# A four-layer sequence of cross-attention and RWKV blocks: ten products of a constant at the start, first queries by seven block products, low-rank projections side by side on TensorE's columns

## The chip, the cores and the metric

The kernel runs on one core of one Trainium2 chip, in fp32 throughout. The metric is the device time of one execution in microseconds. The time before is the median of three runs.

## The reference

The input x has 8 sequences of 112 tokens with 512 channels (896 tokens in all); a context of 375 tokens with 512 channels belongs to each sequence. Four layers follow one another:

```python
# layer 0: one cross-attention without heads
q, k, v = x @ w_q.T, ctx @ w_k.T, ctx @ w_v.T
x = x + alpha * ((softmax(q @ k.T / sqrt(512)) @ v) @ w_o.T)

# layers 1 and 2: RWKV blocks, their states taken from ctx
xa  = LN(x);  sx = shift(xa) - xa
xx  = xa + sx * maa_x
t   = tanh(xx @ maa_w1)              # 512 -> 160, five groups of 32
m   = einsum(t by group, maa_w2)     # five times 32 -> 512
xw, xk, xv, xr, xg = xa + sx * (maa_f + m_f)       # one for each group f
w   = exp(-exp(time_decay + tanh(xw @ decay_w1) @ decay_w2))   # 512 -> 64 -> 512
r, k, v = xr @ Wr.T, xk @ Wk.T, xv @ Wv.T
g   = silu(xg @ Wg.T)
y   = scan over tokens of s = w * s + k v, read out with r     # 32 heads of 16
x   = x + (GN(y) * g) @ Wo.T
x   = x + sigmoid(xr2 @ fWr.T) * (relu(xk2 @ fWk.T)**2 @ fWv.T)

# layer 3: two cross-attentions of 16 heads of 128 channels, then an MLP of 2048
```

## The kernel before, in words

Channels lie on the partitions: x is a tile of 128 partitions by NC = 4 channel groups by N = 896 tokens. A projection is, for each half of the tokens (NH = 448 columns) and each of four output groups, four matmuls of 128x128 weights by 128x448 tokens into one PSUM bank, and an eviction by ACT or DVE. An fp32 matmul shows in the trace as two records.

**Layer 0** (`layer0`, L252) runs in an order written out by hand for PE, DVE, ACT and GpSimd; SyncE's order is chosen by the scheduler. `turned` (L314) transposes w_q and w_k on TensorE, 16 products by an identity each, four to a bank, which ACT and DVE evict in turn from two banks. `product` (L324) then multiplies the two into w_qk, scaled, so that no keys need be made: q0 = w_qk x by `project` (L167, evicted by ACT at L388), and the scores are q0 by the context itself. w_v and w_o are multiplied in the same way into w_vo. The loads go out in the order w_q, w_k, x, context, w_v, w_o. `mean_c` (128x128, all 1/512, a memset of DVE at the start) is the weight of every layer norm's mean (L188).

While that runs, `park` (L279) rearranges the contexts of two sequences into sums of blocks (copies of ACT, subtractions of GpSimd at L291) in a single buffer, tag "blocks", and SyncE puts them into DRAM. From there they are read later by a generator, `values` (L884), which makes layer 3's values: its matmuls `ps_vk` (L994, 0.86 us each, with an ACT eviction each) are work that depends on nothing in layers 1 and 2. `fill(n)` takes n steps from whichever generator is `filler` at the time, so that this work stands in the waits of those layers.

**Layers 1 and 2** (`time_mix_inputs`, L458) go through the two token halves h = 0 and 1. `mixes` makes a layer norm (part_mean and part_var by DVE, `mean_c` by PE, the square by ACT; L184 to L195), the shifted difference sx (GpSimd) and xx, four chunks by DVE at L516. Then come two sets of four matmuls (L525): w1 holds the first four groups of maa_w1 (128 output rows), w1e the fifth group of 32 four times over, filled by four DMAs, so that t1 holds it once on each quarter of the partitions. A Tanh evicts each (t4, t1). The mixing products (L534) have only 32 rows in the contraction, and four of them run beside one another on TensorE's rows; DVE evicts them (L537, L540). `projections` makes d (L552), four matmuls whose weights d1 hold the 64 columns of decay_w1 twice, td by Tanh, then in turn the gate g (L562, Silu at L570) and the decay: ps_w (L579) from td's upper and lower 64 partitions, two products beside one another, e by Exp with a bias (L583) and decay by another Exp (L584). ACT loads a table where it goes from Silu to Exp or back. The tiles e, ruk and the layer norm's part_mean and part_var share the tag "e" with two buffers. After that v, k and r are projected.

The order of this part is found by the scheduler from the program order, dependences and estimated costs. Half 0's projections are the filler of half 1's mixes:

```python
pieces = projections(0, *mixes(0, ...))
values_filler, filler = filler, pieces
following = projections(1, *mixes(1, (2, 1, 2, 1, 1, 1, 0, 0)))
```

`time_mix` is the scan: DVE multiplies and scans, GpSimd multiplies by r, and the sums over the heads' channels (L746) are matmuls with 32 output columns, four of them beside one another on TensorE's columns by `tile_position=(0, 32 * q)`. Fillers stand between them.

**Layer 3** makes its projections by `seven` (L1149): seven products of 2x2 blocks in the place of eight, from sums of blocks of the weights (`weight_sums`) and of the tokens.

Of the kernel before, what the change touches and what calls it, by code (L numbers as in the profile page):

```python
# [30 lines left out]
P = 128  # L31
# [19 lines left out]
BLOCK = 2 * CT  # L51

# [58 lines left out]
def tile_kernel(ctx: ExitStack, tc: tile.TileContext, d: dict, out: bass.AP):  # L111
# [30 lines left out]
    pick = marked.tile([P, 4, 4 * HB], F32, name="pick")  # L142
    mean_c = const.tile([P, P], F32, name="mean_c")
# [89 lines left out]
    def patterns(pool, ident):  # L233
# [10 lines left out]
        nc.vector.tensor_sub(less_mean_h, ident, mean_h)  # L244

# [4 lines left out]


    def layer0():  # L252
# [3 lines left out]
        with (  # L256
# [8 lines left out]
            ident = identity(keep, "a0")  # L265
            w_q, w_k = weight("L0_xattn_w_q"), weight("L0_xattn_w_k")
# [57 lines left out]
            def product(a, b, name, pool, tag, scale=1.0):  # L324

                y = pool.tile([P, NC, C], F32, tag=tag, name=name)
# [55 lines left out]
            with tc.manual_schedule(engines=ORDERED):  # L382
                w_qk = product(turned(w_q, "q"), turned(w_k, "k"), "w_qk", wpool, "w", 1.0 / math.sqrt(C))
                project(
                    ps,
                    w_qk,
                    lambda k, h: halves(x[:, k, :], h),
                    lambda o, h, p: nc.scalar.copy(halves(q[:, o, :], h), p),  # L388
                    "q0",
                )  # L390

                w_vo = product(turned(w_v, "v", wpool, "w"), w_o, "w_vo", last, "w_vo")
# [65 lines left out]
    def time_mix_inputs(n, pre, names, ones_t, first, k, v, r, g, decay, rows):  # L458
# [7 lines left out]
        with (  # L466
# [7 lines left out]
            w1e = one.tile([P, NC, P], F32, name=f"maa1e_{n}")  # L474
# [3 lines left out]
            for q in range(4):  # L478
                part = slice(q * DM, (q + 1) * DM)
                nc.sync.dma_start(w1e[:, :, part], d[pre + "maa_w1"][:, :, P:])  # L480
                nc.sync.dma_start(w2e[part], d[pre + "maa_w2"][P:])
# [24 lines left out]
            def mixes(h, fills):  # L506
# [15 lines left out]
                for dst, w in ((t4, w1), (t1, w1e)):  # L522
                    p = mm(ps, f"ps_t{n}_{h}_{int(dst is t1)}")[:, :NH]
                    for c in range(NC):
                        nc.tensor.matmul(p, w[:, c], xx[:, c, :], start=c == 0, stop=c == NC - 1)  # L525
                    nc.scalar.activation(dst, p, AF.Tanh)
# [21 lines left out]
            def projections(h, xw, xg):  # L548

                p = mm(ps, f"ps_d{n}_{h}")[:, :NH]  # L550
                for c in range(NC):
                    nc.tensor.matmul(p, d1[:, c, :], xw[:, c, :], start=c == 0, stop=c == NC - 1)  # L552
                td = one.tile([P, NH], F32, tag="t4", name=f"td{n}_{h}")
# [21 lines left out]
                for pair in range(2):  # L575
                    ps_w = [mm(ps, f"ps_w{n}_{h}_{o}")[:, :NH] for o in (2 * pair, 2 * pair + 1)]
                    for q in range(2):
# [537 lines left out]
    def weight_sums(pool, tag, w, u, eng=None, later=None):  # L1115
# [22 lines left out]
        for step in steps:  # L1138
            step()
# [667 lines left out]
```

## Time and profile before

| what | value |
| --- | --- |
| runs | 2889.84, 2891.95, 2893.08 us |
| median | 2891.95 us |
| profiled execution | 2892.85 us |
| its span | 2890.7 us |
| mean granted TensorE clock | 0.989 |
| busy: PE, DVE, ACT, POOL | 97%, 62%, 35%, 36% of the span |
| layer 0's first transpose, first w_qk product | 5.79 us, 13.91 us |
| q0 | 27.75 to 51.97 us |
| layer 1: variance of half 1's layer norm | 213.63 us |
| layer 2: the same | 834.28 us |

The span is the profiled execution of one core from its first to its last instruction; the profiled execution's own time holds 2.1 us more around it. Engines are PE (TensorE's matmuls), PEld (its weight loads), DVE, ACT, POOL (GpSimd) and SP (SyncE, which issues the DMAs). A group's line has the source line, the engine, the operation, out and in, the count, and behind the bar the busy time in us, the mean of one in ns, and the idle time ahead of it with what ended it. PEclk is the share of full speed that the clock gate granted to TensorE.

### The profile page before, as it was taken

The page shows a single profiled execution, that of the slowest core. Times are in us where ns is not written, and L with a number is a line of the kernel's source. Part 1 is how long each engine was busy: PE and PEld are TensorE (multiplying, and loading weights), DVE is VectorE, ACT ScalarE, POOL GpSimd, SP SyncE. Part 2 cuts the span into 40 slices and gives each one's busy share as a digit, 9 for nine tenths or more (in the row PEclk, how much of TensorE's full clock was granted, in tenths as well). Part 3 has the DMA queues.
Part 4 walks back from the last instruction along what each step waited for, and adds up shares of the span by engine and source line. Part 5 has one row for each costly group of instructions (what it writes and reads, how often), then busy time and mean ns, then how long its engine had stood idle before and what let it go on. Part 6 is the DMA issues. An engine that isn't in the chain of part 4 may idle for free.

```text
span 2890.7 us, 31049 instructions
## 1 busy us (share of the span) xinstructions
PE 2791.5 (97%) x10476; PEld 1588.2 (55%) x10476; DVE 1800.7 (62%) x2301; ACT 1012.7 (35%) x1953; POOL 1052.2 (36%) x836
## 2 busy tenths in 40 slices
PE   8989999999999999999999999999899999999999
PEld 4734443344444433347467676767476676767544
DVE  1464288856352688834457676757767676757555
ACT  2232466633243456523233232313333232313311
POOL 1432178744231487733322221313122232313030
PEclk9999999999999999999999999999999999999999
DMA  5621498944221789842435352525244352523010
GB/s 206 239 77 39 142 282 254 277 122 136 85 71 57 236 241 277 241 137 92 130 103 156 95 165 94 163 92 159 74 133 133 115 166 89 162 93 115 28 47 26
DMA packets 233310, 400.90 MB, mean 139 GB/s; under 512 B 35144, under 2 KB 170344, under 8 KB 226368
## 3 DMA queue, kind: packets, MB, share of 16 engines
q1 hardware_dynamic: 233152, 398.92, 44.1%
q8 instruction: 84, 1.38, 0.2%
q14 instruction: 74, 0.61, 0.1%
HBM read 321.06 MB, written 77.91 MB: 138 GB/s over the span
## 4 chain that ended last, share of the span: by engine, by line
PE 73%; DVE 15%; POOL 4%; ACT 4%; issue 2%; DMA 2%; SPq 0%; DVEq 0%; ACTq 0%; POOLq 0%
PE ps_vk L994 14%; PE ps_k1k L1235 8%; PE ps_k5k L1235 6%; PE av L1496 4%; PE sc L1448 4%; PE ps_o L167 3%; DVE each L1488 2%; PE ps_k1q L1162 2%; PE ps_fk L167 2%; PE ps_r L562 2%; PE ps_k L562 2%; PE ps_k5q L1162 2%; PE ps_k7q L1162 2%; PE ps_v L562 2%; PE ps_fr L167 2%
## 5 line engine op out<-in xcount | busy, mean ns | idle before, releaser
L994 PE MATMUL ps_vk<-wv,cv 128*128 128x512 f32 x1296 | 583.8, 601 | 15.4 <-ACT k L1092 9.1
L994 PEld LDWEIGHTS ps_vk<-wv,cv 128*128 128x128 f32 x1296 | 243.5, 191 | 339.8 <-issue 285.4
L1483 POOL PARTITION_ALL_REDUCE each<-tops x113 | 182.4, 1614 | 466.0 <-DVE tops L1472 464.1
L1020 POOL TENSOR_TENSOR k<-k,k 128x512 f32<-128x512 f32 (+1 forms) x153 | 197.8, 1293 | 327.0 <-ACT k L1019 276.4
L1458 POOL PARTITION_ALL_REDUCE tops<-top x128 | 139.3, 1088 | 427.5 <-DVE top L1456 417.3
L769 DVE TENSOR_TENSOR_SCAN st<-decay,kv 128x904 f32<-128x904 f32 x128 | 260.7, 2037 | 17.6 <-POOL rs L773 4.4
L773 POOL TENSOR_TENSOR rs<-st,r 128x896 f32<-128x896 f32 x128 | 247.3, 1932 | 51.6 <-DVE st L769 46.7
L1466 ACT ACTIVATE pts<-pts,rests 128x448 f32<-128x448 f32 (+1 forms) x256 | 133.2, 567 | 337.6 <-DVE pts L1464 325.9
L1496 PEld LDWEIGHTS av<-pts,v 125*128 125x128 f32 (+1 forms) x1536 | 190.9, 191 | 33.1 <-ACT pts L1466 3.9
L1448 PEld LDWEIGHTS sc<-q,k 128*128 128x128 f32 x1536 | 189.4, 192 | 33.0 <-DVE each L1488 9.4
L1448 PE MATMUL sc<-q,k 128*128 128x112 f32 x1536 | 193.0, 276 | 8.6 <-DVE each L1488 8.3
L1488 DVE RECIPROCAL each<-each 128x224 f32<-128x224 f32 x113 | 174.7, 1546 | 31.3 <-POOL each L1483 28.7
L1496 PE MATMUL av<-pts,v 125*128 125x112 f32 (+1 forms) x1536 | 190.9, 274 | 1.3 <-ACT pts L1466 1.3
L1235 PE MATMUL ps_k1k<-cs,wsk 128*128 128x375 f32 x480 | 173.6, 483 | 6.5 <-ACT u2k L1237 5.3
L765 DVE TENSOR_TENSOR kv<-vp,k 128x904 f32<-128x904 f32 x128 | 141.5, 1105 | 60.5 <-ACT vp L667 55.3
L1019 ACT COPY k<-ps_vk 128x512 f32<-128x512 f32 (+1 forms) x153 | 89.2, 583 | 179.6 <-PE ps_vk L994 176.8
L1092 ACT COPY k<-ps_vk 128x512 f32<-128x512 f32 (+1 forms) x153 | 89.1, 583 | 172.9 <-PE ps_vk L994 163.7
L1456 DVE TENSOR_REDUCE top<-sc 128x224 f32<-128x672 f32 x128 | 109.1, 852 | 28.6 <-PE sc L1448 28.6
L667 ACT COPY vp<-vj 128x896 f32<-128x896 f32 x124 | 112.8, 910 | 9.3 <-DMA vj<-rows 5.4
L1464 DVE TENSOR_TENSOR pts<-sc,tops 128x672 f32<-128x672 f32 x128 | 102.8, 803 | 17.6 <-POOL tops L1458 17.6
L1235 PEld LDWEIGHTS ps_k1k<-cs,wsk 128*128 128x128 f32 x480 | 84.0, 189 | 51.3 <-ACT u2k L1237 7.6
L1237 ACT COPY p1k<-ps_k1k 128x375 f32<-128x375 f32 x60 | 27.9, 465 | 212.1 <-PE ps_k1k L1235 212.1
(416 smaller groups left out, 4788.6 us busy)
## 6 DMA issues: line engine op xcount, KB each, us to landing
vj<-rows SPq DMA_DIRECT2D x124, 448.0 KB
cv<-blocks SPq DMA_DIRECT2D x181, 251.5 KB
cs<-blocks SPq DMA_DIRECT2D x120, 375.0 KB
wvs<-k SPq DMA_DIRECT2D x128, 256.0 KB
v<-wvs SPq DMA_DIRECT2D x128, 256.0 KB
cx<-in_ctxT SPq DMA_DIRECT2D x38, 750.0 KB
v<-wvs SPq DMA_DIRECT2D x128, 126.0 KB
wvs<-k SPq DMA_DIRECT2D x64, 224.0 KB
```

Source lines behind the costliest of these rows:

```text
L167: nc.tensor.matmul(p, w[:, k, o * P : (o + 1) * P], rhs(k, h), start=k == 0, stop=k == NC - 1)
L562: nc.tensor.matmul(y, ws[f][:, c, o * P : (o + 1) * P], x_f, start=c == 0, stop=c == NC - 1)
L769: nc.vector.tensor_tensor_scan(flat(st), flat(decay[:, c]), flat(kv), 0.0, ALU.mult, ALU.add)
L773: nc.gpsimd.tensor_mul(by_batch(rs), st[:, :, :L], by_batch(r[:, c, :]))
L994: nc.tensor.matmul(to, left, right, start=start and n == 0, stop=k == 1, skip_group_check=True)
L1020: nc.gpsimd.tensor_add(y, z, y)
L1162: nc.tensor.matmul(to, lhsT, rhs, start=start and k == 0, stop=k == 1, skip_group_check=not start)
L1235: nc.tensor.matmul(y, lhsT, rhs, start=start and k == 0, stop=k == 1, skip_group_check=True)
L1448: nc.tensor.matmul(sc[:, t, y * L : (y + 1) * L], kt[:, o, t * CT : t * CT + P], q[:, o, b * L : (b + 1) * L], start=True, stop=True,)
L1483: nc.gpsimd.partition_all_reduce(each, it[4], P, ReduceOp.add)
L1488: nc.vector.reciprocal(each, sums)
L1496: nc.tensor.matmul(av[:, y], v[:nt, t, y * HD : (y + 1) * HD], pts[:nt, t, y * L : (y + 1) * L], start=t == 0, stop=t == 2,)
```

## The change

There are six edits.

- Ten matmuls of mean_c by mean_c into a PSUM bank that nothing reads stand first on PE.
- q0 is made by `seven` in the place of `project`. The token sums lie in z (free until the attention), the weight sums in w_vo (filled only afterwards), and p1, u2, u3 in a tile `parts0` of the tag "blocks". `seven` and its helpers move up in the file; `weight_sums` takes a tile, and `tile_of` a function, for that.
- A tile `folded` holds the sum of the identity's four column quarters: 128 rows by 32 columns.
- w1e holds the fifth group once (one DMA). Each of the four channel chunks' products goes to a column tile of 32 columns of its own, and so to its own quarter of the partitions of one bank; ACT copies them, and four products with `folded` on four column tiles sum the chunks and repeat the sum on each quarter; Tanh follows. They stand ahead of t4's four matmuls and after them.
- d is made on two column tiles of 64 columns, each with one half of the 448 tokens, so that td has 224 columns with the first tokens above and the last below.
- ps_w takes four products of 224 columns in the place of two of 448 for each pair of channel groups, and each Exp at L583 becomes two of 224 columns.

```diff
+START = 10
...
+    folded = marked.tile([P, DM], F32, name="folded")
...
+        nc.vector.tensor_add(folded, ident[:, :DM], ident[:, DM : 2 * DM])
+        for q in range(2, 4):
+            nc.vector.tensor_add(folded, folded, ident[:, q * DM : (q + 1) * DM])
...
             ident = identity(keep, "a0")
+            start = mm(ps, "ps_start")
+            for _ in range(START):
+                nc.tensor.matmul(start[:, :P], mean_c, mean_c, start=True, stop=True)
...
                 w_qk = product(turned(w_q, "q"), turned(w_k, "k"), "w_qk", wpool, "w", 1.0 / math.sqrt(C))
-                project(
+                b11, b21, b12, b22 = quarters(x)
+                t0, t1, t2, t3 = quarters(z)
+                nc.vector.tensor_sub(t0, b12, b11)
+                nc.vector.tensor_sub(t1, b22, t0)
+                nc.vector.tensor_sub(t2, b22, b12)
+                nc.vector.tensor_sub(t3, b21, t1)
+                w_vo = last.tile([P, NC, C], F32, tag="w_vo", name="w_vo")
+                parts = work.tile([P, 3, BLOCKS, 2, CT], F32, tag="blocks", name="parts0", bufs=1)
+                parts = parts.rearrange("p c j k s -> p (c j k s)")
+                room = {"p1": (0, 1), "u2": (2, 4), "u3": (3, 5)}
...
+                    if y is None:
+                        nc.scalar.copy(dst, p)
+                    else:
+                        nc.vector.tensor_add(dst, p, y)
...
+                sums = weight_sums(None, w_vo, w_qk, "q0", nc.vector)
+                for _ in seven(
                     ps,
+                    lambda what, m: parts[:, room[what][m] * NH : (room[what][m] + 1) * NH],
                     w_qk,
...
+                product(turned(w_v, "v", wpool, "w"), w_o, "w_vo", None, None, y=w_vo)
...
-            w1e = one.tile([P, NC, P], F32, name=f"maa1e_{n}")
+            w1e = one.tile([P, NC, DM], F32, name=f"maa1e_{n}")
+            nc.sync.dma_start(w1e, d[pre + "maa_w1"][:, :, P:])
...
-                nc.sync.dma_start(w1e[:, :, part], d[pre + "maa_w1"][:, :, P:])
...
-                for dst, w in ((t4, w1), (t1, w1e)):
-                    p = mm(ps, f"ps_t{n}_{h}_{int(dst is t1)}")[:, :NH]
-                    for c in range(NC):
-                        nc.tensor.matmul(p, w[:, c], xx[:, c, :], start=c == 0, stop=c == NC - 1)
-                    nc.scalar.activation(dst, p, AF.Tanh)
+                p = mm(ps, f"ps_t{n}_{h}_1")[:, :NH]
+                for c in range(NC):
+                    part = slice(c * DM, (c + 1) * DM)
+                    nc.tensor.matmul(p[part], w1e[:, c], xx[:, c, :], start=True, stop=True, tile_position=(0, c * DM))
+                nc.scalar.copy(t1, p)
+                p = mm(ps, f"ps_t{n}_{h}_0")[:, :NH]
+                for c in range(NC):
+                    nc.tensor.matmul(p, w1[:, c], xx[:, c, :], start=c == 0, stop=c == NC - 1)
+                nc.scalar.activation(t4, p, AF.Tanh)
+                p = mm(ps, f"ps_t{n}_{h}_2")[:, :NH]
+                for q in range(4):
+                    part = slice(q * DM, (q + 1) * DM)
+                    nc.tensor.matmul(p[part], folded, t1, start=True, stop=True, tile_position=(0, q * DM))
+                nc.scalar.activation(t1, p, AF.Tanh)
...
-                p = mm(ps, f"ps_d{n}_{h}")[:, :NH]
+                p = mm(ps, f"ps_d{n}_{h}")[:, : NH // 2]
                 for c in range(NC):
-                    nc.tensor.matmul(p, d1[:, c, :], xw[:, c, :], start=c == 0, stop=c == NC - 1)
-                td = one.tile([P, NH], F32, tag="t4", name=f"td{n}_{h}")
+                    for q in range(2):
+                        part = slice(q * DD, (q + 1) * DD)
+                        nc.tensor.matmul(
+                            p[part],
+                            d1[:, c, part],
+                            xw[:, c, q * NH // 2 : (q + 1) * NH // 2],
+                            start=c == 0,
+                            stop=c == NC - 1,
+                            tile_position=(0, q * DD),
+                        )
+                td = one.tile([P, NH], F32, tag="t4", name=f"td{n}_{h}")[:, : NH // 2]
...
-                    ps_w = [mm(ps, f"ps_w{n}_{h}_{o}")[:, :NH] for o in (2 * pair, 2 * pair + 1)]
-                    for q in range(2):
-                        part, o = slice(q * DD, (q + 1) * DD), 2 * pair + q
-                        nc.tensor.matmul(ps_w[q], d2[part, o * P : (o + 1) * P], td[part], start=True, stop=True)
-                    for q in range(2):
-                        o = 2 * pair + q
+                    ps_w = [mm(ps, f"ps_w{n}_{h}_{pair}_{q}")[:, :NH].rearrange("p (y s) -> p y s", y=2) for q in range(2)]
+                    for y in range(2):
+                        for q in range(2):
+                            part, o = slice(q * DD, (q + 1) * DD), 2 * pair + y
+                            nc.tensor.matmul(
+                                ps_w[q][:, y],
+                                d2[part, o * P : (o + 1) * P],
+                                td[part],
+                                start=not y,
+                                stop=True,
+                                skip_group_check=True,
+                            )
+                    for y in range(2):
+                        o = 2 * pair + y
                         e = work.tile([P, NH], F32, tag="e", name=f"e{n}_{h}_{o}")
-                        nc.scalar.activation(e, ps_w[q], AF.Exp, bias=vec(pre + "time_decay", o))
+                        for q in range(2):
+                            part = e[:, q * NH // 2 : (q + 1) * NH // 2]
+                            nc.scalar.activation(part, ps_w[q][:, y], AF.Exp, bias=vec(pre + "time_decay", o))
                         nc.scalar.activation(
                             decay[:, o, h * BH : (h + 1) * BH, 1:], by_batch(e), AF.Exp, scale=-1.0
                         )
```

`seven` as it is called here, moved and with `tile_of` as said (cut to its products):

```python
for m in range(2):
    product(first[m], m, lambda k: w[:, k], b11)
    nc.scalar.copy(p1[m], first[m])
for m in range(2):
    product(first[m], m, lambda k: w[:, 2 + k], b21, start=False)
    put(0, m, first[m], None)
for m in range(2):
    product(p, m, lambda k: s()[1][:, k], t[1])
    nc.vector.tensor_add(u2, p, p1[m])
    product(p, m, lambda k: s()[2][:, k], t[2])
    nc.vector.tensor_add(u3, p, u2)
    product(q, m, lambda k: s()[0][:, k], t[0])
    put(1, 2 + m, q, u3)
    product(p, m, lambda k: w[:, 2 + k, 256:], t[3], start=False)
    put(0, 2 + m, p, u2)
    product(q, m, lambda k: s()[3][:, k], b22, start=False)
    put(1, m, q, u2)
```

## The prediction

> **What bounds the kernel now.** I read the busy shares and the chain of waits first, then the granted clock and busy time by stage, then the groups of the lines that the change touches, and last the timeline around each of them.
>
> ```profile
> span 2890.7 us, 31049 instructions
> PE 2791.5 (97%) x10476; PEld 1588.2 (55%) x10476; DVE 1800.7 (62%) x2301; ACT 1012.7 (35%) x1953; POOL 1052.2 (36%) x836
> PE 73%; DVE 15%; POOL 4%; ACT 4%; issue 2%; DMA 2%; SPq 0%; DVEq 0%; ACTq 0%; POOLq 0%
> ```
>
> TensorE is busy 97% of the span, but the chain is on PE for only 73%: in some stages PE only keeps itself filled while another engine sets the pace. So I ask stage by stage.
>
> ```profile
> 165.00:200.00 35.00, 31.18 (x81) 13.11 (x81) 26.81 (x34) 7.92 (x12) 23.82 (x23) 0.85 0.21 62
> 240.00:300.00 60.00, 58.84 (x167) 26.52 (x166) 24.07 (x36) 16.16 (x24) 14.53 (x13) 0.94 0.13 45
> 300.00:370.00 70.00, 70.00 (x178) 33.34 (x176) 23.83 (x20) 28.74 (x50) 17.89 (x12) 1.00 0.56 171
> 780.00:850.00 70.00, 65.92 (x191) 28.14 (x190) 40.98 (x54) 32.55 (x47) 27.64 (x26) 1.00 0.24 77
> ```
>
> The columns are length, busy PE, PEld, DVE, ACT, POOL, granted clock, DMA share, GB/s. The first row is layer 1's first token half: PE has 3.8 us of holes and only 0.85 of its clock. In the second half (from 240) and the tail before time_mix (300 to 370) PE has almost no hole, so work taken from PE there shortens the run. Layer 2 repeats this from 780, with the clock at 1.00.
>
> ```profile
> L167 PE MATMUL ps_q<-x,w_qk 128*128 128x448 f32 x64 | 24.2, 539 | 0.0
> L525 PE MATMUL ps_t<-xx,maa 128*128 128x448 f32 x32 | 14.3, 563 | 4.2 <-DVE xx L516 4.2
> L525 PE MATMUL ps_t<-xx,maa1e 128*128 128x448 f32 x32 | 12.7, 539 | 0.0
> L552 PE MATMUL ps_d<-xw,d 128*128 128x448 f32 x32 | 12.7, 539 | 0.0
> L746 PE MATMUL ps_y<-rs,pick 128*32 128x448 f32 x512 | 58.0, 545 | 3.3 <-POOL rs L773 3.3
> ```
>
> These are busy us, mean ns, then idle before. Every fp32 matmul is two records, so the first row is 32 matmuls of 448 columns in 24.2 us: 0.75 us each. The last row is the one place that already uses four column tiles: 256 matmuls, 64 groups of four, 58.0/64 = 0.91 us a group. Its tiles start 0.02 us apart, and a group takes one matmul's 0.75 us plus some 0.1 us at each change into and out of the tiling.
>
> **Part 1, ten products of mean_c at the start.**
>
> ```profile
> 5.79 1.94 PE L320 MATMUL ps_tq<-ident_a,w_L_xattn_w_q_None 128*128 128x128 f32 x8 [5.79 <-DMA w_L_xattn_w_q_None<-in_L_xattn_w_q]
> 13.91 2.41 PE L330 MATMUL ps_w_qk<-t_k,t_q 128*128 128x512 f32 x5
> ```
>
> PE waits 5.79 us for w_q, then 32 transposes run until 13.9, most at 0.21 us; from 13.4 on a transpose takes 0.107. Ten 128-column products at the cold 0.21 us a pass are 20 x 0.213 = 4.3 us. They wait only for a memset that ends at 1.0, so they end about 5.4, under the wait for w_q. If they raise the clock, the transposes are paced by their PSUM evictions (0.59 us ACT, 0.69 us DVE, in turn on two banks), and w_qk starts near 11.6: -2.2 us, at best -2.7, at worst 0. In the trace the clock rose at 13.4 while transposes were all that PE had run. The Trainium skill, "TensorE: Matmul & The Clock Gate", Part 1, has the gate judge windows of about 3.4 us; by that the 4.3 us of products may straddle two windows, fill neither, and bring nothing.
>
> **Part 2, q0 by seven products.** 28 matmuls for 32: -4 x 0.752 = -3.0 us. Beside them DVE gains 4 subtractions of tokens (during t_k and w_qk, when it is idle), 4 sums of weights between w_qk's last eviction and the third product (they need about 1.2 us for the first; 8 matmuls = 6 us cover them), and 10 evictions of 0.6 to 0.7 us, one per 1.5 us of PE: hidden. What is moved: parts0 takes the only "blocks" buffer, so park(1)'s 8 GpSimd subtractions (7.2 us, before at 23.3) wait until about 47, and SyncE issues their puts before Wg's load. Wg was issued at 54.71 and landed at 59.54, and ACT has its two turning copies (1.04 us each) queued ahead of w_vo's evictions. Wg now lands near 60 and both copies stand before the third eviction: 0 to 2 us of PE stall, taken as 0.5. Part 2: -2.5.
>
> **Part 3, fewer loads.** w1e goes from 4 DMAs to 1 per layer, and folded costs three tiny DVE adds: SyncE and DVE are idle there, nothing.
>
> **Part 4, the fifth group of the low-rank projection.** Before, 8 matmuls of 0.752 = 6.0 us for t4 and t1. After: four column tiles (0.75), t4 (3.0), four folded column tiles (0.75), some four changes (0.4): 4.9, so -1.1 us of PE each of four times. But the first quartet stands ahead of t4 and needs all four xx chunks, which DVE makes one by one: t4 used to run under that wait. The last chunk was ready at 175.24, 237.39, 794.35 and 856.56. Worked out from there (4 x 0.752 for t4, two quartets, changes), the mixing products start later by 0.1 (layer 1, first half), 0.75 (layer 1, second), 0.85 and 0.8 us (layer 2). So it costs, where PE's sum says it gains. If the tiles ran at 3.07 times one, as the Trainium skill's "TensorE: Matmul & The Clock Gate", Part 3, has for four row tiles, each quartet would take 0.98 us, 1.8 us more over all eight; L746 shows four together, and I go by that.
>
> **Part 5, the decay projection d.** 4 matmuls of 448 become 8 of 224 in two column tiles: 3.0 to 1.5 + 0.2, so -1.3 us each time.
>
> **Part 6, ps_w.** Four 224-column products for two of 448 per pair, row tiles as before: 0 (bounds 0 to +0.25 per pair by weight loads). Every exponential is split in two: 0.63 us becomes two of about 0.40 (estimate between the 0.63 of 448 columns and the 0.376 of a 112-column ACTIVATE), +0.17 us of ACT.
>
> **Part 7, a new order on ACT.** The program order of the changed kernel shows what the diff doesn't: in the first half of each layer, the second decay exponential no longer follows its e at once, but a table load, g1's Silu and another table load. Before:
>
> ```profile
> 210.36 0.64 ACT L583 ACTIVATE e<-ps_w,vecs 128x448 f32<-128x448 f32 x1
> 211.03 0.58 ACT L584 ACTIVATE decay<-e 128x448 f32<-128x448 f32 x1
> 211.62 1.28 ACT L570 ACT_TABLE_LOAD   x1
> 211.64 0.62 DVE L184 TENSOR_TENSOR part_var_ln<-sq_ln 128x448 f32<-128x448 f32 x1 [7.45 <-ACT decay L584]
> 212.92 0.54 ACT L570 ACTIVATE g<-ps_g 128x448 f32<-128x448 f32 x1
> 213.63 1.02 PE L188 MATMUL var_ln<-part_var_ln,mean_c 128*128 128x448 f32 x2 [2.96 <-DVE part_var_ln L186]
> ```
>
> part_var shares the two "e" buffers, so it waits for that decay, and PE waits for part_var (3 us idle). After, the decay stands behind 1.28 + 0.54 + 1.28 = 3.1 us more, plus 2 x 0.17: part_var, the variance, the second half's whole layer norm are 3.4 us later. Ahead of it the mixing starts later (0.1 or 0.85 from part 4, and 1.7 for two filler products that now stand before it) and d is 1.3 shorter: +0.5 in layer 1, +1.2 in layer 2. So var_ln is +3.9 and +4.6 us. Three more fillers (ps_vk, 0.858 each, 2.6 us) stand ahead of it, which are then missing from the 100% busy tail: net +1.3 and +2.0. The last filler pair's eviction is itself an ACT copy behind the displaced decay, so PE stands still there for 4 to 6 us instead of 3. In layer 1 the clock had already dropped after the 3 us wait (half speed from 214.6 to 218.1, costing 1.7 us); in layer 2 it had not, and will: +1.7, bounds 0 to 3.4.
>
> **The sum.** Layer 0: -2.2 - 2.5 = -4.7. Layer 1, first half: +1.3; d's saving is in it already. Second half, where PE is nearly gapless: +0.75 - 1.3 = -0.55. Layer 2: +2.0 + 1.7 = +3.7, then +0.8 - 1.3 = -0.5. Layer 3 is unchanged. Together -0.75, say -0.7. The profiled execution took 2892.85 us (2.1 around its span), 0.9 above the median of the three runs: 2892.15 on its scale, 2891.3 on the median's. About 0.2%, 5.8 us, is what a measurement of this kernel can tell from no change, so I forecast no change.
>
> **Rivals.** (A) All PE work saved reaches the end: -2.2 - 3.0 - 4 x 1.1 - 4 x 1.3 = -14.8, or -10 with parts 4 and 5 by half; 2877 to 2882, near 2880. For it: 97% busy, and filler can close holes. Against it: the waits on xx and on the decay, which no PE saving shortens. (B) Slower: the displaced decay exponential decides. If the filler ahead of var_ln isn't given back in the tail (+2.6 per layer: the first sums of time_mix had only 5 us between rs ready at 365.06 and PE at 370.08) and a second cold window follows in each layer (+1.7 each), that is +8.6, so about +8: 2900. It decides from the point where PE stands still for over 6 us ahead of var_ln in both layers. (C) The columns don't run side by side: a quartet costs 3.0, not 0.75, and d 3.0, not 1.5: +18 + 6 = +24, 2915; L746 speaks against it. (D) The start brings nothing because the clock falls again or never rises: +2.2, 2893.5, inside the forecast.
>
> **How the numbers follow.** Forecast with D: 0.45. A: 0.29. B: 0.24. C: 0.02. The forecast's own range is 2886 to 2897: Wg's stall (0 to 2), cold windows (0 to 3.4), the start (-0.5 to +2.2). The range goes on into A and B, 2880 to 2900, and leaves out what lies beyond (about 0.08 of A, 0.12 of B and C). Faster by over 0.2% is A and the end of the forecast, 0.31; slower is B and C, 0.26; the rest 0.43.
>
> **What would show it.** Right: transposes of w_q 0.107 us apart and w_qk near 11.6; ps_q at 21 us of PE; part_var released by a decay behind g1's Silu near 215.5; idle before var_ln of 4 to 6 us and a clock below 1.00 after it in both layers; d at 1.5 us. Wrong: a decay that follows its e at once on the chip, so that var_ln stays at its place; PE waiting for ACT's copies of Wg in layer 0; a wait before the first ps_y.

## The result, and the profile after

| | median, us | runs | ratio to before | 95% interval |
| --- | --- | --- | --- | --- |
| before | 2891.22 | 20 | 1 | |
| changed | 2896.23 | 20 | 1.0016 | 1.0009 to 1.0023 |

The changed kernel is slower by 0.16%, 4.6 us (0.0016 x 2891). That lies within the 0.2% that the prediction calls no change, and within its range, but the interval is clear of 1, and it moved the other way than the small gain that the sum had. The profiled execution of the changed kernel took 2895.32 us, 2.5 more than that of before.

First the page of the changed kernel: span, busy time by engine, and the chain that ended last.

```profile
span 2893.5 us, 31304 instructions
...
PE 2792.0 (96%) x10584; PEld 1584.8 (55%) x10584; DVE 1819.2 (63%) x2322; ACT 1013.0 (35%) x1969; POOL 1052.3 (36%) x836
...
PE 71%; DVE 15%; POOL 5%; ACT 5%; issue 2%; DMA 2%; SPq 0%; DVEq 0%; ACTq 0%; POOLq 0%
```

PE is as busy as before (2792.0 us against 2791.5), although four products of q0, and most of t1 and d, should be gone: the ten products at the start take 4.6 us of it, and t4 and t1 together, as will be seen, take more than before. The chain is on PE for 71% instead of 73%, on GpSimd and ACT for 1% more each.

The windows of before again, of the changed kernel (length, busy PE, PEld, DVE, ACT, POOL, granted clock, DMA share, GB/s):

```profile
165.00:200.00 35.00, 30.80 (x97) 11.20 (x96) 25.90 (x33) 6.26 (x11) 21.34 (x22) 0.85 0.13 39
240.00:300.00 60.00, 58.38 (x188) 26.63 (x188) 24.04 (x36) 15.06 (x26) 14.72 (x13) 0.94 0.11 40
300.00:370.00 70.00, 70.00 (x186) 33.61 (x186) 24.00 (x21) 31.52 (x54) 16.95 (x11) 1.00 0.57 162
780.00:850.00 70.00, 63.06 (x200) 25.10 (x199) 37.68 (x46) 30.79 (x49) 29.34 (x27) 0.95 0.26 80
```

The first half of layer 2 has lost what it had: PE is busy 63.06 us instead of 65.92, at a clock of 0.95 instead of 1.00. The tail from 300 on is as full as before. The same view, narrowed to the 13 and 14 us around the second half's variance in layer 1 and in layer 2, of before:

```profile
209.00:222.00 13.00, 10.04 (x23) 4.05 (x22) 1.87 (x3) 9.62 (x15) 0.00 (x0) 0.87 0.21 67
832.00:846.00 14.00, 11.72 (x32) 5.65 (x33) 2.35 (x4) 10.21 (x14) 0.00 (x0) 1.00 0.17 64
```

and of the changed kernel:

```profile
209.00:222.00 13.00, 8.35 (x21) 3.96 (x22) 1.88 (x3) 8.00 (x15) 1.27 (x1) 0.74 0.31 99
832.00:846.00 14.00, 9.28 (x23) 3.87 (x22) 2.82 (x3) 8.68 (x16) 1.40 (x1) 0.76 0.23 71
```

The clock given up there (one minus the granted clock, times the length) is 1.7 us in layer 1 and nothing in layer 2 before, and 3.4 us in each layer after.

The timeline of PE at the start:

```profile
1.04 4.63 PE L373 MATMUL ps_start<-mean_c 128*128 128x128 f32 x20 [1.04 <-DVE eps L148]
5.78 1.27 PE L428 MATMUL ps_tq<-ident_a,w_L_xattn_w_q_None 128*128 128x128 f32 x8
...
11.83 1.55 PE L438 MATMUL ps_w_qk<-t_k,t_q 128*128 128x512 f32 x3
```

The ten products end at 5.7 us under the wait for w_q, the next eight transposes take 1.27 us instead of 1.94, and w_qk starts at 11.83 instead of 13.91. From there to the first transpose of w_v (46.72, before 51.80) the kernel gains another 3.0 us: q0 does what was said of it. Next, from the timeline of ACT and PE, the load of Wg:

```profile
61.52 1.99 ACT L626 COPY turng<-w_L_xattn_Wg_None 128x1024 f32<-128x1024 f32 x2 [4.33 <-DMA w_L_xattn_Wg_None<-in_L_xattn_Wg]
...
64.06 1.19 PE L460 MATMUL ps_r<-ident_a,cx 128*125 128x128 f32 x8 [0.64 <-ACT w_vo L441]
```

Wg lands at 61.52 (before 59.54), the two turning copies hold up the third and fourth evictions of w_vo, and PE waits 0.64 us for them.

The groups of t1 and d (busy us, mean ns, idle before with what ended it):

```profile
L661 PE MATMUL ps_t<-xx,maa 128*128 128x448 f32 x32 | 13.4, 555 | 0.0
...
L657 PE MATMUL ps_t<-xx,maa1e 128*32 128x448 f32 x32 | 12.0, 551 | 4.7 <-DVE xx L648 4.7
...
L695 PE MATMUL ps_d<-xw,d 128*64 128x224 f32 x64 | 8.4, 413 | 0.0
...
L666 PE MATMUL ps_t<-t,folded 128*32 128x448 f32 x32 | 3.8, 551 | 0.0
```

d fell from 12.7 to 8.4 us over its four places. The last row, the quartets with `folded`, is what four tiles side by side cost: 3.8/4 = 0.95 us each. The first quartets (L657) cost 12.0 us, 3.0 each, hardly less than the 12.7 us of the full matmuls that they replace. The timeline of PE in layer 1's second half shows why. Before:

```profile
235.33 3.17 PE L525 MATMUL ps_t<-xx,maa 128*128 128x448 f32 x8
238.34 3.17 PE L525 MATMUL ps_t<-xx,maa1e 128*128 128x448 f32 x8
241.44 0.64 PE L534 MATMUL ps_mw<-t,maa 32*128 32x448 f32 x1
```

The changed kernel, with DVE's line for xx first:

```profile
234.68 4.95 DVE L648 SCALAR_TENSOR_TENSOR xx<-sx,vecs,xa 128x448 f32<-128x448 f32 x4
...
237.58 0.95 PE L657 MATMUL ps_t<-xx,maa1e 128*32 128x448 f32 x4
238.90 1.73 PE L657 MATMUL ps_t<-xx,maa1e 128*32 128x448 f32 x4 [0.37 <-DVE xx L648]
240.56 3.27 PE L661 MATMUL ps_t<-xx,maa 128*128 128x448 f32 x8
243.76 0.96 PE L666 MATMUL ps_t<-t,folded 128*32 128x448 f32 x8
244.65 1.98 PE L1154 MATMUL ps_vk<-wv,cv 128*128 128x512 f32 x4
246.56 0.64 PE L675 MATMUL ps_mw<-t,maa 32*128 32x448 f32 x1
```

The quartet's eight records do not start together. DVE hands out xx's chunks one after another (at 236.00, 237.42, 238.84 and 239.63). PE is free at 237.58, and from there each column tile starts when its own chunk is there: two tiles at 237.58, one at 238.90, one at 239.69. That is three steps in turn. t4, which before ran under the same wait, now starts only behind them at 240.56. From the first record to the first mixing product it is 8.98 us, where before it was 6.11; 1.91 of the 2.87 more are a pair of fillers. Fillers come back later: in both kernels, layer 1 up to its first sum of time_mix holds 88 records of ps_vk, 14 ahead of the second half's variance and 74 behind it before, 20 and 68 after.

Last, the timeline of ACT, DVE and PE ahead of the second half's variance in layer 1, with the displaced decay (sq is the square that ACT makes of xa):

```profile
202.30 1.70 ACT L197 ACTIVATE sq_ln<-xa 128x1792 f32<-128x1792 f32 x1 [4.97 <-DVE xa L195]
...
208.59 0.78 ACT L743 ACTIVATE e<-ps_w,vecs 128x224 f32<-128x224 f32 x2
...
209.40 1.28 ACT L720 ACT_TABLE_LOAD   x1
210.69 0.54 ACT L720 ACTIVATE g<-ps_g 128x448 f32<-128x448 f32 x1
211.25 1.28 ACT L744 ACT_TABLE_LOAD   x1
...
212.55 0.58 ACT L744 ACTIVATE decay<-e 128x448 f32<-128x448 f32 x1
213.03 0.57 ACT L1266 COPY k<-ps_vk 128x512 f32<-128x512 f32 x1
213.16 0.62 DVE L186 TENSOR_TENSOR part_var_ln<-sq_ln 128x448 f32<-128x448 f32 x1 [10.89 <-ACT decay L744]
...
213.65 3.78 PE L1154 MATMUL ps_vk<-wv,cv 128*128 128x512 f32 x4 [4.87 <-ACT k L1266]
...
217.22 1.23 PE L190 MATMUL var_ln<-part_var_ln,mean_c 128*128 128x448 f32 x2
```

The order is the predicted one: e, a table load, g1's Silu, a table load, and only then the second decay, at 212.55. part_var starts when it ends. The last line but one is what the sum had not priced: the third pair of fillers, whose PSUM bank ACT frees only behind the decay, stands ahead of var_ln on PE and runs at half clock, 3.57 us for what takes 1.71. var_ln, whose sums were ready at 215.1, starts at 217.22. The line of sq before, where it started 7.42 us ahead of part_var (10.86 after):

```profile
204.22 1.70 ACT L195 ACTIVATE sq_ln<-xa 128x1792 f32<-128x1792 f32 x1 [2.64 <-DVE xa L193]
```

### The profile page after: what moved, and what is told of

Read it like the earlier page. It is cut to its first block, busy times and chain, and to the rows that moved or that the text cites. A ratio compares the mean times of both kernels' runs of the same rounds, so it can differ in the third digit from the quotient of the medians.

```text
span 2893.5 us, 31304 instructions
## 1 busy us (share of the span) xinstructions
PE 2792.0 (96%) x10584; PEld 1584.8 (55%) x10584; DVE 1819.2 (63%) x2322; ACT 1013.0 (35%) x1969; POOL 1052.3 (36%) x836
## 4 chain that ended last, share of the span: by engine, by line
PE 71%; DVE 15%; POOL 5%; ACT 5%; issue 2%; DMA 2%; SPq 0%; DVEq 0%; ACTq 0%; POOLq 0%
PE ps_vk L1154 13%; PE ps_k1k L1303 8%; PE ps_k5k L1303 6%; PE av L1560 4%; PE sc L1512 4%; PE ps_o L169 3%; DVE each L1552 2%; PE ps_k1q L306 2%; PE ps_k5q L306 2%; PE ps_k7q L306 2%; PE ps_fk L169 2%; PE ps_r L712 2%; PE ps_k L712 2%; PE ps_fr L169 2%; PE ps_fv L169 1%
## 5 line engine op out<-in xcount | busy, mean ns | idle before, releaser
L1154 PE MATMUL ps_vk<-wv,cv 128*128 128x512 f32 x1296 | 587.6, 603 | 23.9 <-ACT k L1252 11.0
L1180 POOL TENSOR_TENSOR k<-k,k 128x512 f32<-128x512 f32 (+1 forms) x153 | 197.9, 1294 | 364.1 <-ACT k L1179 258.8
L925 DVE TENSOR_TENSOR kv<-vp,k 128x904 f32<-128x904 f32 x128 | 141.5, 1105 | 50.2 <-ACT vp L827 44.1
```

What stands on the lines that cost most here:

```text
L925: nc.vector.tensor_mul(flat(kv), flat(vp), flat(k[:, c]))
L1154: nc.tensor.matmul(to, left, right, start=start and n == 0, stop=k == 1, skip_group_check=True)
L1180: nc.gpsimd.tensor_add(y, z, y)
```

## The experiments

Marks of the traces in us. "Layer 0" is the time to t4's or t1's first product of layer 1; "layer 1" and "layer 2" run from that product to the first sum of time_mix, and "var_ln" from it to the second half's variance. The ratio is to the runs of before that were made beside it.

| kernel | ratio | interval | layer 0 | layer 1 (var_ln) | layer 2 (var_ln) |
| --- | --- | --- | --- | --- | --- |
| before | 1 | | 170.7 | 199.4 (42.9) | 198.4 (44.5) |
| before again | | | 172.5 | 199.3 (42.9) | 199.4 (44.5) |
| changed | 1.0016 | 1.0009 to 1.0023 | 167.1 | 202.7 (50.2) | 206.3 (51.9) |
| changed again | | | 165.7 | 204.7 (50.1) | 206.1 (51.9) |
| e1 changed, decay pinned | 1.0010 | 1.0001 to 1.0019 | 165.7 | 198.3 (43.8) | 203.3 (47.1) |
| e2 without d | 1.0001 | 0.9992 to 1.0010 | 165.8 | 199.9 (44.6) | 202.9 (46.4) |
| e3 without t1 | 0.9985 | 0.9976 to 0.9993 | 168.3 | 199.7 (48.1) | 200.8 (49.9) |
| e4 start and q0 alone | 0.9988 | 0.9980 to 0.9997 | 167.9 | 198.5 (43.0) | 200.2 (44.5) |
| e7 without t1, pinned | 0.9976 | 0.9967 to 0.9985 | 168.2 | 197.6 (43.4) | 199.4 (44.9) |
| e9 changed, t4 first | 0.9974 | 0.9966 to 0.9982 | 168.6 | 196.9 (47.2) | 198.4 (49.5) |
| e6 t4 first, pinned | 0.9970 | 0.9959 to 0.9982 | 166.3 | 195.9 (42.3) | 197.9 (44.9) |
| e8 t1 late, without d | 0.9980 | 0.9971 to 0.9989 | 166.4 | 198.0 (43.9) | 195.8 (45.5) |
| e5 t1 late, pinned | 0.9965 | 0.9952 to 0.9978 | 166.7 | 193.6 (43.7) | 194.3 (45.9) |
| e10 as e5, no start | 0.9968 | 0.9956 to 0.9981 | 169.3 | 192.9 (43.6) | 194.3 (45.9) |

**Two more traces.** The first question to any difference of 2 us is what moves without a change.

> The kernel before once more, for a second trace. Every theory expects the same time; what it shows is how much a mark moves from run to run without any change: if the windows of half clock fall differently, by up to 1.7 us each, and nowhere else.

> The changed kernel once more, for a second trace. var_ln of layer 1 should again come 3 to 4 us later than before and the first quartet of the second half take about 3 us; the windows of half clock may fall elsewhere.

They took 2891.03 and 2891.81 us, one run each. In the changed kernel's second trace var_ln of layer 1 stands at 215.81 us, 2.2 later than in the first trace of before where 3 to 4 were expected (7.2 if both are counted from the layer's first product), and that half's first quartet spreads over 4.5 us up to t4's first product, where the first trace has 3.0. Two windows of the kernel before, of its first trace and of its second:

```profile
100.00:115.00 15.00, 13.35 (x92) 10.81 (x91) 8.60 (x15) 6.75 (x15) 8.48 (x9) 1.00 0.54 191
685.00:700.00 15.00, 14.63 (x31) 6.45 (x32) 14.79 (x14) 2.89 (x5) 10.99 (x9) 0.89 0.53 170
```

```profile
100.00:115.00 15.00, 12.57 (x72) 10.24 (x71) 7.88 (x13) 6.05 (x12) 7.95 (x9) 0.89 0.57 204
685.00:700.00 15.00, 12.21 (x29) 5.07 (x28) 14.68 (x11) 5.30 (x10) 13.41 (x12) 1.00 0.48 149
```

The third number from the end is the granted clock. A window of half clock lies near 688 us in the first trace and near 109 us in the second, and the other way round there is none. Each costs up to 1.7 us, so single marks of the same kernel differ by almost 2 us (the first product of layer 1 at 170.69 and 172.53). Where no window moved, the stages agree to 0.06 us: 199.39 and 199.33 for layer 1, 42.94 and 42.89 for its var_ln. So the traces say where, and the medians of many runs say how much.

**Pinning the decay.** The first theory was the displaced decay.

```diff
-                    nc.scalar.activation(e, p, AF.Silu)
+                    silu = nc.scalar.activation(e, p, AF.Silu)
+                    if behind is not None:
+                        tc.add_manual_dep(silu.ins, behind.ins.name, ..., reason="decay first")
...
-                    gated(1 + pair)
+                    gated(1 + pair, last)
```

> The changed kernel with one order pinned: g1's and g2's Silu may not stand on ACT ahead of the decay exponentials of their pair. Nothing is computed differently. Theory (the displaced decay is the loss): in layer 1 the second decay starts right after its e, about 3.1 us earlier than the 212.55 us of the changed kernel, part_var of the second half starts near 210 instead of 213.16, and var_ln follows near 212.3 instead of 217.22; in layer 2 var_ln comes about 5 us earlier than 840.99. Some 1.7 us of filler per layer goes back to the tail, so each layer gains about 3.3 us and the run comes to about 2889.6 us, 6.6 below the changed kernel's median of 2896.2. Rival (the wait of the first column quartet and the filler ahead of the mixing products are the loss): var_ln moves, but the mixing of the second half absorbs it, and the run stays within 2 us of 2896.

The timeline of this kernel, ACT, DVE and PE:

```profile
206.82 0.58 ACT L751 ACTIVATE decay<-e 128x448 f32<-128x448 f32 x1
...
207.43 0.62 DVE L186 TENSOR_TENSOR part_var_ln<-sq_ln 128x448 f32<-128x448 f32 x1 [7.75 <-ACT decay L751]
...
209.52 0.99 PE L190 MATMUL var_ln<-part_var_ln,mean_c 128*128 128x448 f32 x2 [3.33 <-DVE part_var_ln L188]
```

The decay is back behind its e, and var_ln comes 43.8 us after the layer's first product instead of 50.2. But the run is only 0.06% (plus or minus 0.11) below the changed kernel's ratio: 1.7 us of the expected 6.6, and by the interval under 5. The theory has its mechanism, and at most a part of the loss. In this one trace the two layers are 8 us shorter than in the mean of the changed kernel's two, but behind them it is 7 us longer: 422.0 us from layer 1's first sum of time_mix to layer 2's first product (419.3 and 418.2), and 1900.5 from layer 2's first sum to the end (1898.1 and 1895.3). The last stage alone differs by 4.7 us between the two traces of before, so what takes the 8 us back stays open.

**Taking the parts away.** In e2, d, ps_w and their exponentials are as before; in e3, t4, t1 and w1e; in e4 both.

```diff
# e2, against the changed kernel (e4 has both hunks)
-                    for q in range(2):
-                        ...
-                        nc.tensor.matmul(p[part], d1[:, c, part], ..., tile_position=(0, q * DD))
+                    nc.tensor.matmul(p, d1[:, c, :], xw[:, c, :], start=c == 0, stop=c == NC - 1)
# e3
-                    nc.tensor.matmul(p[part], w1e[:, c], xx[:, c, :], ..., tile_position=(0, c * DM))
-                ...
+                for dst, w in ((t4, w1), (t1, w1e)):
+                    ...
+                        nc.tensor.matmul(p, w[:, c], xx[:, c, :], start=c == 0, stop=c == NC - 1)
```

> The changed kernel with d, ps_w and their exponentials as before (no column tiles there, no split Exp); start, seven products and t1 by columns stay. Theory (displaced decay): the scheduler's order has each decay right behind its e again, so only the 2.2 us later mixing in each first half is left of the loss; var_ln of layer 1 near 212 instead of 217.22, that of layer 2 some 5 us earlier than 840.99; layer 0's -3.6, layer 1 about +1.0, layer 2 about +1.6 against the kernel before: about 2890 us, although d is 1.3 us longer four times. Rival (t1 by columns is the loss): still 2895 to 2897 us.

> The changed kernel with t4 and t1 as before (eight full matmuls, four loads of w1e); start, seven products, d by columns and the split Exp stay. Theory (displaced decay): the decay still stands behind g1's Silu, so var_ln in each layer is 5 us later than before against the start of its layer, about 2 us of which t1 by columns had added in the changed kernel; given back in part by three fillers and by d: layer 1 +1.6, layer 2 +3.3 with a second cold window, layer 0 -3.6: about 2892.5 us. Rival (t1 by columns is the loss): layers 1 and 2 gain d's 1.3 us per half, about 2885 us.

> Only the ten products at the start and q0 by seven products; layers 1 and 2 as before. Both theories: layer 0 ends 3.6 us earlier (first product of o0 at 119.7 instead of 123.3 us), and if nothing later takes it back, 2887.6 us. What it tells: whether a gain in layer 0 reaches the end. If the filler or a DMA later takes it, 2890 to 2891 us.

The start and q0 alone are worth 3.5 us at the end (e4, plus or minus 2.5), of some 4 us in layer 0. With d as well it is 0.9985 (e3): the displaced decay is still there, var_ln is 5.1 us later than in e4, and nothing of it shows at the end: behind var_ln the stage up to the first sum is 3.9 and 4.8 us shorter than in e4, with three fillers less in it and d's shorter products. With t1 instead it is 1.0001 (e2), with both 1.0016. So t1 costs 0.0013 without d and 0.0031 with it (plus or minus 0.0012 each), some 4 and 9 us. d with its decay costs nothing that shows without t1 (e3 against e4), and 0.0015 (plus or minus 0.0011) beside it, some 4 us. So neither theory has both runs: e3's 2886.11 us is near the rival's 2885, e2's 2891.38 near the displaced decay's 2890. That each costs more beside the other than alone is not settled by these intervals.

**The order of t4 and the quartet.** If t1 is the larger loss, is it the tiles or their place? e9 makes this one exchange, e6 the same with the pin of e1.

```diff
+                p = mm(ps, f"ps_t{n}_{h}_0")[:, :NH]      # t4: four matmuls and their Tanh
+                ...
                 p = mm(ps, f"ps_t{n}_{h}_1")[:, :NH]      # the first quartet
                 ...
-                p = mm(ps, f"ps_t{n}_{h}_0")[:, :NH]
-                ...
```

> The changed kernel with the decays pinned ahead of the Silu, and t4's four matmuls ahead of the first quartet instead of behind it; the quartets stay ahead of the mixing products. Theory (the place): t4 runs under the wait for the xx chunks again, the quartet then runs its four tiles side by side in 0.75 us instead of 2.98 (layer 1, second half of the changed kernel), so the mixing of each half starts about 1 to 2 us earlier than with the quartet first; some 3 us less than the pinned kernel's +2.3 against before: about 2889 us. Rival (tiles by themselves): the quartet takes as long behind t4 as ahead of it, about 2892 us.

> The changed kernel with one thing undone: t4's four matmuls stand ahead of the first quartet. The decay stays where the changed kernel has it, behind g1's Silu. Theory (the quartet's place is the larger loss): the mixing of each half starts 1 to 2 us earlier and the quartet takes 0.75 us; about 9 us of the changed kernel's 5 above before come off: 2886 us, some 3 above the 2883.0 us with the decays pinned as well. Rival (the displaced decay is the larger loss and hides the quartet's): var_ln of layer 1 stays near 217 us and the run above 2891 us.

The timeline of PE in e9, layer 1's second half, and the groups of t4 and of the first quartet:

```profile
235.72 3.17 PE L656 MATMUL ps_t<-xx,maa 128*128 128x448 f32 x8
238.82 0.96 PE L661 MATMUL ps_t<-xx,maa1e 128*32 128x448 f32 x8
239.71 1.98 PE L1154 MATMUL ps_vk<-wv,cv 128*128 128x512 f32 x4
241.63 0.96 PE L666 MATMUL ps_t<-t,folded 128*32 128x448 f32 x8
242.52 0.64 PE L675 MATMUL ps_mw<-t,maa 32*128 32x448 f32 x1
```

```profile
L656 PE MATMUL ps_t<-xx,maa 128*128 128x448 f32 x32 | 14.1, 558 | 4.2 <-DVE xx L648 4.2
...
L661 PE MATMUL ps_t<-xx,maa1e 128*32 128x448 f32 x32 | 3.8, 551 | 0.0
```

Behind t4 all four chunks are there, and the quartet's eight records are one block of 0.96 us. All four quartets take 3.8 us instead of 12.0. With this one exchange the run falls from 1.0016 to 0.9974, by 0.42% (plus or minus 0.11), 12 us; 2883.82 us, where 2886 was expected. In the traces layers 1 and 2 together are 14.6 us shorter than in the mean of the changed kernel's two. Counted from xx's last chunk the mixing starts 1.5 to 2.2 us earlier each time, 8.1 in all. The rows of t4 and t1 add up to 21.7 us of PE (14.1, and 3.8 for each set of quartets) against 29.2 in the changed kernel and 27.0 before, PE is idle for 2.8 us less, and half clock lasts 27.3 us in the two layers instead of 37.5, worth 5.1 at most. The decay is displaced as ever, and var_ln 4.3 and 5.0 us later than before: so a late var_ln is not by itself what the changed kernel loses. Pinned as well (e6) it is 0.9970, 2883.0 us where 2889 was expected; against e9 that is no difference that these runs resolve. All three pairs (e1, e7, e6 against the same kernel unpinned) lean the same way, by 0.0006, 0.0009 and 0.0004.

**d pinned, and t1 later still.** In e5 the whole making of t1 stands behind the mixing products of the first four groups, as only g's read it; e7 and e8 are its parts, d pinned without t1's tiles, and t1 late without d.

```diff
# e5 (with the pin of e1); e8 moves the same lines, beside the hunk of e2; e7 is e3 with the pin of e1
-                p = mm(ps, f"ps_t{n}_{h}_1")[:, :NH]      # ahead of t4
-                ...
-                nc.scalar.copy(t1, p)
                 ...
-                p = mm(ps, f"ps_t{n}_{h}_2")[:, :NH]      # behind t4
-                ...
-                nc.scalar.activation(t1, p, AF.Tanh)
                 ...
+                p = mm(ps, f"ps_t{n}_{h}_1")[:, :NH]      # all of it, behind the four groups
+                ...
+                nc.scalar.activation(t1, p, AF.Tanh)
                 mixed([("g", c) for c in range(NC)], w2e, t1)
```

> Start, seven products and d by columns; t1 as in the kernel before; the decays pinned ahead of the Silu. Theory: the displaced decay still costs something where t1 is as before (var_ln of layer 1 stood at 216.33 us against 210.81 without d), but two thirds of it come back as filler that the tail no longer holds; so pinning gains 1 to 3 us on the 2886.1 us of the same kernel unpinned: about 2884 us. Rival (the displaced decay costs nothing in the end, all of it comes back): 2886 us as without the pin.

> Start, seven products, and t1 by columns moved behind the mixing products; d, ps_w and the exponentials as in the kernel before. Theory (the place): t1's PE time of 3.0 us becomes 1.5 four times, and counts where PE is gapless (the two second halves): 3 us below start and seven products alone (2886.6), about 2883.5 us. Rival (tiles by themselves): at or above 2886.6 us.

> The changed kernel with the decays pinned ahead of the Silu, and with the whole making of t1 (both quartets, the copy, the Tanh) moved behind the mixing products of the first four groups, just ahead of those of g that read it. Theory (the place of the quartets is the loss: ahead of t4 their tiles wait for DVE's xx chunks one by one and run as three steps of 0.75 us instead of one, and the mixing starts late): behind the mixing both quartets take 0.75 us each, t1 costs 1.5 us of PE instead of 3.0 where it is gapless, and the mixing no longer waits for it; with start, seven products and d the run comes to about 2881 us, 9 below the kernel before. Rival (column tiles cost by themselves, by their changes of mode and the lost overlap, wherever they stand): about 2887 us, no better than start and seven products alone.

e7 reached 0.9976, 2885.95 us: the rival's 2886, though its ratio is 0.0009 below that of e3. e8 reached 0.9980 (0.9971 to 0.9989), 2885.61: of the 3 us expected below e4, 2.3 (plus or minus 3.6) by the ratios. e5 has 0.9965 (0.9952 to 0.9978), 2882.35 us, within 1.4 us of the theory's 2881. It is 10 us faster than before and the fastest of all; against e6 and e9 the intervals overlap.

**Without the ten products.**

```diff
# against e5
-            start = mm(ps, "ps_start")
-            for _ in range(START):
-                nc.tensor.matmul(start[:, :P], mean_c, mean_c, start=True, stop=True)
```

> The fastest version so far (t1 behind the mixing, decays pinned) without the ten products at the start. Theory: the transposes of w_q and w_k run at half clock again, w_qk starts at 13.9 us instead of 11.8, and all of the 2.1 us reaches the end: about 2884.5 us against 2882.4. Rival: a later wait (the load of Wg, x) takes it back: 2882.4 us.

It reached 0.9968 (0.9956 to 0.9981), against 0.9965 with them. In the trace w_qk starts at 13.47 us and the mark stays 1.9 us late up to the first sum of time_mix (362.25 against 360.34), but the two ratios can't tell 2 us from none. That the start's 2 us reach the end is not shown.

## Why the prediction was wrong

The step that failed most is Part 4's price for the first quartet, 0.75 us of PE where it takes 3.0; beside it, Part 7 has var_ln only half as late as it came. Both are in layers 1 and 2.

**Layer 0 held.** The start brought -2.1 us and q0 -3.0, as worked out; the copies of Wg cost 0.6 instead of 0.5. Over all traces with these parts layer 0 lies at 165.7 to 168.6, before at 170.7 and 172.5: -4.6 in the mean, -4.7 predicted. e4 shows 3.5 of it at the end (plus or minus 2.5).

**Part 7 had the mechanism, and its size was off.** Layers 1 and 2 together are 409.9 us in the mean of the changed kernel's two traces and 398.3 in that of before: +11.6, where the sum had +1.3 - 0.55 + 3.7 - 0.5 = +4. (By the ratios, which rest on more runs, the changed kernel against e4 is +8, plus or minus 3.) In those traces PE is idle for 18.0 and 18.9 us in the two layers, before 10.5 and 12.1, and runs at half clock for 37.5 us in both, before 27.3 and 23.9. Most of the 7.6 us by which the traces exceed the sum are in the step to var_ln.

Predicted were +3.9 us for var_ln in layer 1 and +4.6 in layer 2; against the layer's first product both traces have +7.2 and +7.4. In layer 1 there are three terms. ACT's detour itself was 3.44 us (sq to part_var 10.86, before 7.42), where 3.4 was predicted. The late mixing and the shorter d were summed to +0.5 ahead of it; it is +1.7 (from the layer's first product to sq 35.23 us, before 33.53), because sq waits for DVE, which comes from the mixing over xg to xa, and d is not on that path: its 1.3 us were credited to a chain that they are not in. And the filler pair ahead of var_ln, named in the prediction but priced only as idle time, adds 2.07 us by running at half clock in front of it. The two missing terms are 3.3 of the 7.6 us, and layer 2's excess of 2.8 (7.4 - 4.6) comes on top.

Half clock was underpriced as well: around var_ln the clock given up is 1.7 us more than before in layer 1, where the sum had nothing, and 3.4 in layer 2, where it had 1.7. So this step of the sum has little more than half of what came: "d is 1.3 shorter: +0.5 in layer 1, +1.2 in layer 2. So var_ln is +3.9 and +4.6 us". But pinning the decay, which takes back 6.3 of the 7.2 us in layer 1, brought 1.7 us at the end (e1), and d taken away altogether 4 us (e2), where the exchange of t4 and the quartet brought 12 (e9). So this is not the step that weighs most.

**Part 4 weighs most: it priced the wait nearly right and the work wrong.** Counted from the first product, the mixing starts later by 0.3 and 1.0 to 2.5 us in layer 1 and 1.0 and 0.7 in layer 2, without the filler pairs; 0.1, 0.75, 0.85 and 0.8 were predicted. But "four column tiles (0.75)" is not what PE was busy with: the first quartet takes 3.0 us, since each tile goes when its own chunk comes. t4 and t1 together were to take 1.1 us less of PE each time, and take 0.5 more (29.2 us against 27.0 over four); in e9, with the quartet behind t4, they take 1.3 less (21.7). The prediction had the row that shows it, PE waiting for DVE's xx at L525, and took from it when the last chunk came, not that the tiles would be taken apart. That row also held the remedy, t4 under the wait; e9 shows that it was worth 12 us, more than the whole loss. In the sum Part 4 is +2.5 us of later mixing; by the ratios t1 costs 4 us without d and 9 with it, plus or minus 3.5. How that cost divides between PE's work, the wait and half clock, and how much of it needs the displaced decay beside it, stays open.

**The signs and the range.** Nearly all that the prediction named as signs of being right came: w_qk near 11.6, the decay behind g1's Silu, 4.87 us of idle PE ahead of the filler pair in front of var_ln, a clock below 1.00 there in both layers. d at 1.5 us did not (2.1), and one sign of being wrong came as well, PE's wait for the copies of Wg, at 0.64 us. None of them looked at the quartet. That 2896.23 us still lies within 2886 to 2897 is partly luck, as that margin was for Wg's load, half clock and the start.

**Part 5** was nearly right: d saves 1.1 us each time (12.7 to 8.4 over four) in the changed kernel, and 1.5 in e9 (6.9 over four). **Part 6** cost nothing on PE (8.7 to 8.2 us), and each half Exp takes 0.38 us (12.3 over 32), 0.40 predicted.

**The rivals.** B, slower by the displaced decay, had the sign and half of its conditions: a second window of half clock did follow in each layer (the granted clock of 0.74 and 0.76 above), but the fillers came back, and e3 and e9 have the displaced decay and are faster than before. A had 2877 to 2882 with all of the PE time saved, which the changed kernel did not reach; e5, another kernel, in which the tiles do run side by side and the decay is pinned, came to 2882. C, columns that don't run side by side, was dismissed by the sums of time_mix. It was true of the first quartet and not of the second, for a reason that those sums do not have: their four inputs are there when they start.

**The rules.** The trace has 0.95 us for four tiles whose inputs are ready, near one matmul's 0.75, and 3.0 us, in the mean of four, where they are not. The Trainium skill, "TensorE: Matmul & The Clock Gate", Part 3, gives a factor of 3.07 for four row tiles; no factor describes the second of these cases. In the trace, half clock comes in stretches such as that of 685 to 700 us above (0.89 of 15 us, so 3.3 us at half), which agrees with the window of about 3.4 us in Part 1 of that page. What the prediction let it say, that the ten products may straddle two windows and bring nothing, did not happen: the clock rose at 3.9 to 6.9 us in every trace with them and at 11.4 to 13.5 us in the three without.

## What to carry to other kernels

Before small matmuls are laid side by side, look at when each one's operand is ready: tiles that come one by one behind a producer run one by one, and they hold up whatever had used that wait. Put the full matmuls under the producer's wait, and the tiles behind them. Ask of each saving whether the chain that sets the stage runs through the engine that saves; and where a wait gets longer, count the half clock that may follow it as well as the wait: fillers come back later in the stage, that does not.

## What the runs showed of the hardware

The granted clock falls in windows that move from run to run of the same kernel, and one window is worth up to 1.7 us; two traces of the kernel before have them near 688 us and near 109 us, with the stages between equal to 0.06 us. Ten products of a constant, 4.6 us, raised the clock at 3.9 to 6.9 us in eleven traces; with the transposes alone it rose at 11.4 to 13.5 us in three. Four column tiles with ready operands take 0.95 us, with the changes of mode at either end; the same four behind a producer that hands out its chunks 0.8 to 1.8 us apart (mostly 1.42) keep TensorE busy for 3.0 us in the mean. Half clock does not go by the length of a wait alone: around waits of TensorE of 4.87 and 4.72 us ahead of var_ln, both traces of the changed kernel have 6.8 us of it in each layer, and e9, with the same waits, has 3.4.
